# A two-layer graph attention kernel on one NeuronCore: layer 2's unit in another order (scores, hub values, turned exponentials, row turns)

## The chip, the cores and the metric

The kernel runs on one core of a Trainium2 chip. The metric is the device time of one execution in microseconds (us), the median of several. The engines are PE (TensorE, matmuls; PEld is its weight load), DVE (VectorE), ACT (ScalarE), POOL (GpSimd) and SP (SyncE, which here only issues DMAs). Each engine works through its own list of instructions in program order and waits on semaphores for the others.

## The reference

Eight graphs with the same 2048 nodes and the same links `adj`, 64 features a node. Two attention layers: in the first each of four heads maps x, in the second one head maps the leaky result. Each layer's scores are products of the mapped rows with themselves, masked by the links:

```python
mask = graph + jnp.eye(N) > 0
def gat(h, mask, b):                       # h: [..., N, D]
    s = jnp.where(mask, jnp.einsum('...nd,...md->...nm', h, h), -1e16)
    return jnp.einsum('...nm,...md->...nd', softmax(s), h) + b
h = jnp.einsum('bnc,hdc->bhnd', x, Wh)
z = leaky_relu(cat_heads(gat(h, mask, bh)), 0.2)
h2 = jnp.einsum('bnk,dk->bnd', z, Wo)
z2 = leaky_relu(gat(h2, mask, bo), 0.2)
out = (z2 - mu) * rsqrt(var + 1e-5) * gamma + beta
return layernorm(x + out)
```

## The kernel before, in words

The links are few: node 0 and its neighbours (the first 59 nodes, the "hub") have many, all others few. The other 1989 nodes are put into 153 sets of 13. For each set the kernel finds up to 128 nodes that any of its 13 members links to, and gathers just their rows from a table in HBM. Layer 1 does this from x, layer 2 from the table of second maps that layer 1 writes.

Layer 2 (lines 1319 to 1577) works in 39 units: unit 0 has one set, every other unit four. One pass of the loop `for u in range(-3, NU + 6)` is called unit u here. What it issues, in the order of the code:

- `values2` (line 1373, PE, "values"): the weighted sums of unit u, from the gathered rows and the masked weights `es2` (named share in the profile). Two units share a bank `o2`: the odd one begins it, the even one ends it.
- `gathers(u + LEAD)` (line 872, POOL): the indirect DMAs of the rows of unit u+9, into the buffers that the values of unit u have read. 36 buffers, four gathers a unit.
- the first part of `norm_sets` (lines 1401 and 1403, DVE), only after an even unit: reciprocals of the sums and the product. Its later parts (`spread`) go to fixed places of the next six units, either at `work_on(u, 0)` or at `work_on(u, 1)`: an odd unit gets leaky (1408), mean (1412), centring (1421), a variance (1436) and the products 1442, 1446, 1447; an even unit a mean, a centring, a product and a variance.
- `turn_scores(u + 1)` (line 1354, PE, "turned exponentials"): four transposes of the exponentials into the bank `turned_e`.
- `keep_scores(u + 1)` (line 1362, DVE, "masked weights"): the product of the turned exponentials and the links, into `es2`.
- `hub_step(k)` (PE 1174 the hub's scores, DVE 1183 the subtraction of its mask, ACT 1186 its exponentials, PE 1197 the hub's values of the step before). It has steps up to unit 5 only.
- `turn2(u + 3)` in two halves (line 560 on PE, "row turns", and line 1497 on ACT, "row copies"): each gathered row tile is transposed into one of three banks `t` and copied to `xts`.
- `scores2(u + 2)` between the halves (line 1343, PE, "scores", into `bank0`; line 1346, ACT, the exponentials `eT`). It reads the four row copies of unit u+2 and the own maps `bd`.
- `catch_up` (ACT): what the norms have left for ACT, the squares (1418) of the centred rows and the two steps of a reciprocal root (1428, 1429).
- `spread_own(u + 3)` (line 1137, ACT, "own maps"): two copies of the own nodes' maps into `bd`, at the unit's end.

SP loads the table of x + beta (1392) and stores the results, twelve DMAs a norm (1461). No planner sets the order: it is the order of the calls.

Of the kernel before, what the change touches and what calls it, by code (L numbers as in the profile page):

```python
# [361 lines left out]
def fast_kernel(ctx: ExitStack, tc: tile.TileContext, x, adj, Wh, bh, Wo, bo, gamma, beta, out, flag):  # L362
# [4 lines left out]
    H, D, _ = Wh.shape  # L367
# [17 lines left out]
    NHB = (NS + S10 - 1) // S10  # L385
# [38 lines left out]
    def half(k):  # L424
        return slice(k * 64, (k + 1) * 64)
# [4 lines left out]
    def sums(p):  # L430

        return slice(p * K1, (p + 1) * K1)
# [21 lines left out]
    NV = (NS + 7) // 8  # L454
# [152 lines left out]
    def hub_sets(b):  # L607

        return b * S10, min(S10, NS - b * S10)
# [254 lines left out]
    def pair(s):  # L864
        return 0 if s == NS - 1 else (s + 2) // 2
# [118 lines left out]
    def nodes(v, ap, tile):  # L984

        four = tile.rearrange("(t n) b d -> n t b d", n=32)
        for a in range(2):
            s = 8 * v + 4 * a
            w = min(4, NS - s)
            if w <= 0:  # L990
                continue
            for t in range(4):
                p0 = t * 32 + a * SET
                rest = ap[2 * (t % 2) + t // 2::4, BASE:, :].rearrange("f (k s) c -> k f s c", s=NS)[1:, :, s:s + w, :]
                yield (tile[p0 + 1:p0 + SET].rearrange("p (f w) c -> p f (w c)", f=2)[:, :, :w * D],
                       rest.rearrange("k f s c -> k f (s c)"))
            for s1, node, n in firsts(s, w):
                for t in range(2):
                    k0 = s1 - s
                    yield (four[a * SET][2 * t:2 * t + 2].rearrange("u (f w) c -> u f (w c)", f=2)[:, :, k0 * D:(k0 + n) * D],  # L1000
                           ap.rearrange("(f u v) n c -> v u f (n c)", f=2, u=2)[t, :, :, node * D:(node + n) * D])
# [112 lines left out]
    def one(name, tag):  # L1114
        return psum1.tile([P, 2, 512], F32, tag=tag, name=name)
# [4 lines left out]
    NU = (NS + 3) // 4  # L1120
# [3 lines left out]
    def side(u):  # L1124
        return (u - 1) % 2 if u else 0
# [6 lines left out]
    def spread_own(u):  # L1132

        w = len(sets[u])
        for p in range(2):
            src = own[half(p), :, sets[u][0] * SET:(sets[u][0] + w) * SET]
            nc.scalar.copy(bd[u % 3][half(p), :w, :, 16 * p:16 * p + SET], src.rearrange("c q (k n) -> c k q n", k=w))
# [27 lines left out]
    def hub_scores2(k, sp):  # L1165
        b = hub_order[k]
        n = BASE if b == NHB else hub_sets(b)[1] * SET
        held["sh", k] = sp
        for q in range(Q):
            if b == NHB:  # L1170
                keys = ownh[:, q // 2, q % 2 * HUB:q % 2 * HUB + n]
            else:
                keys = own[:, q, b * S10 * SET:b * S10 * SET + n]
            nc.tensor.matmul(sp[:n, q * 2 * HUB:(q + 1) * 2 * HUB], keys, ownb[:, q, :, :].rearrange("c p n -> c (p n)"),
                             start=True, stop=True)

    def hub_lift2(k):
        b = hub_order[k]
        n = BASE if b == NHB else hub_sets(b)[1] * SET
        sp = held.pop(("sh", k))  # L1180
        e = esh[k % 2]
        m = maskh[:n, 0, :].rearrange("p (k h) -> p k h", h=H)[:, :, 0] if b == NHB else maskt[:n, b, :]
        nc.vector.tensor_tensor(e[:n, :Q * 2 * HUB].rearrange("p (a n) -> p a n", a=2 * Q),
                                sp[:n, :Q * 2 * HUB].rearrange("p (a n) -> p a n", a=2 * Q),
                                m.unsqueeze(1).to_broadcast([n, 2 * Q, HUB]), OP.subtract)
        nc.scalar.activation(e[:n, :Q * 2 * HUB], e[:n, :Q * 2 * HUB], AF.Exp, bias=shifts[:n, 1:2], scale=1.0)

    def hub_values2(k):
        b = hub_order[k]
        first, last = k == 0, k == NHB  # L1190
        n = BASE if b == NHB else hub_sets(b)[1] * SET
        e = esh[k % 2]
        rw = rows.pop(("h", k))
        for q in range(Q):
            for p in range(2):
                c0 = (2 * q + p) * HUB
                nc.tensor.matmul(oh2[half(p), q * W2 + p:q * W2 + p + K1], e[:n, c0:c0 + 64], rw[:n, q, sums(p)],
                                 start=(first and q == 0), stop=last, skip_group_check=True)

    def hub_step(k, sp):  # L1200
        if k <= NHB:
            hub_scores2(k, sp)
            hub_lift2(k)
        if 0 < k <= NHB + 1:
            hub_values2(k - 1)

    def clear_esh():
        for k in range(2):
# [9 lines left out]
    for i in range(-3, NG + 3):  # L1218
        if 0 <= i + 1 < NG:
            sp = one(f"s{i + 1}", "S")  # L1220
# [17 lines left out]
        if 0 <= i < NG:  # L1238
            op = one(f"o{i}", "O")
# [5 lines left out]
        if NG - LOOK <= i < NG - 1:  # L1245
            for j in range(2):
                k = 2 * (i - NG + LOOK) + j
# [65 lines left out]
    def bank2(name, tag, bufs=1):  # L1313
        return psum2.tile([P, 2, 512], F32, tag=tag, name=name, bufs=bufs)
# [6 lines left out]
    def bank1(name):  # L1321
        return psum2.tile([P, 512], F32, tag="T", name=name, bufs=3)
# [13 lines left out]
    def scores2(u):  # L1336

        w = len(sets[u])
        sp = bank[0].rearrange("p (k n) -> p k n", k=4)
        for k, s in enumerate(sets[u]):  # L1340
            xt = held["T", 2, pair(s)].rearrange("c j (q n) -> c j q n", q=Q)
            for q in range(Q):
                nc.tensor.matmul(sp[q * 32:(q + 1) * 32, k, :], bd[u % 3][:, k, q, :], xt[:, s % 2, q, :], start=True, stop=True,  # L1343
                                 tile_position=(0, q * 32))
        e = held["E", u] = late.tile([P, 4, P], F32, tag="eT", name=f"eT{u}", bufs=2)
        nc.scalar.activation(e[:, :w], sp[:, :w], AF.Exp, bias=shifts[:, 1:2], scale=1.0)
# [109 lines left out]
    def norm_sets(v, op):  # L1456
        w = min(4, NS - 8 * v)

        def store(y):
            for src, dst in nodes(v, out, y):  # L1460
                nc.sync.dma_start(out=dst, in_=src)  # L1461

        view = op[:, :, :4 * W2].rearrange("p f (w c) -> p f w c", w=4)[:, :, :w]
        return norm(f"s{v}", v, view[:, :, :, 1:1 + D], view, 2 * w, store, NV - 4 <= v < NV - 2)
# [12 lines left out]
    def spread(u, parts, ahead=True):  # L1477

        for k, part in enumerate(parts):
            for t in range(2):  # L1480
                at = jobs.setdefault((u + k, t), [])
                if k == 0 and ahead:
                    at[:0] = part[t]
                else:
                    at.extend(part[t])
# [37 lines left out]
    k = 9  # L1523
    spread_own(0)
    for u in range(-3, NU + 6):
        if 0 <= u < NU:
            a = side(u)
            if a == 0:
                op = bank2(f"o2_{u}", "O")
            values2(op, sets[u], es2[a], a, len(sets[u + 1]) if a == 0 and u else 0)  # L1530
            if u + LEAD < NU:
                gathers(u + LEAD)
            if u == 0:
                nc.vector.memset(es2[0][:, :, :1, SET:2 * SET], 0.0)
            if a == 1 or u == 0:
                parts = norm_sets((u - 1) // 2 if u else NV - 1, op)
                for job in parts[0][0]:
                    job()
                spread(u + 1, parts[1:], False)
        if u == NU - 1:  # L1540
            range_of(1, rall2)
            in_limits()
        if 0 <= u + 1 < NU:
            turn_scores(u + 1)
            a = side(u + 1)
            keep_scores(u + 1, a)
        if u in (NU, NU + 1, NU + 3):
            last = jobs.pop((u, 1), [])
            n = 1 if u == NU + 1 else len(last)
            jobs[u, 0] = last[:n] + jobs.get((u, 0), [])  # L1550
            jobs[u, 1] = last[n:]
            catch_up()
        work_on(u, 0)
        for _ in range(2 if u == -3 else 1):
            if k <= NHB + 1:
                hub_step(k, bank1(f"sh{k}") if k <= NHB else None)
                if 8 <= k - 1 and k + 5 <= NHB:
                    hub_block(k + 5, hrows[(k - 1 - 8) % 6])
                if k == NHB + 1:
                    spread(u + 2 - u % 2, norm_hub(oh2))  # L1560
                k += 1
        if u + 3 < NU:
            turn2(u + 3, sets[u + 3][:2])
        if 0 <= u + 2 < NU:
            scores2(u + 2)
        catch_up()
        if u + 3 < NU:
            turn2(u + 3, sets[u + 3][2:])
        work_on(u, 1)
        if 3 <= u + 3 < NU:  # L1570
            spread_own(u + 3)
        if u == -2:
            range_of(0, rall)
            lists_fit()
# [40 lines left out]
```

## Time and profile before

| what | us |
|---|---|
| median of 3 runs (lowest, highest) | 963.1 (962.69, 968.35) |
| span of the profiled execution, first to last instruction | 828.9 |
| what lies around it, against the median | 134.2 |
| layer 2, from the first gather to the end | 575.9 to 828.9 |

The page does not give the profiled execution's own device time; its span is set against the median. In a row of the timeline stand the start and the length in us, the engine, the line, the operation, output<-input, a shape and the count; in brackets the idle time of the engine just before it and what ended it. A row of the stretches has the length, then the busy time (and instructions) of PE, PEld, DVE, ACT and POOL, the granted clock of PE (1.00 is full), the busy share of the DMA engines and GB/s.

### The profile page before, as it was taken

How to read it: one execution, taken by the hardware profiler on the slowest of the kernel's cores; microseconds unless marked ns; L12 is line 12 of the kernel's file. 1: busy time of each engine (PE TensorE's matmuls, PEld its weight loads, DVE VectorE, ACT ScalarE, POOL GpSimd, SP SyncE). 2: the span in 40 equal slices, each digit the busy share in tenths (PEclk: the TensorE clock that was granted, in tenths of full speed). 3: DMA queues.
4: the chain of work that ended last, by engine and by line, in shares of the span. 5: the costliest groups of instructions: out<-in, count | busy, mean ns of one | idle time of the engine just before them, and what ended most of it. 6: DMA issues, size and time to landing. Idle time of an engine off the chain costs nothing.

```text
span 828.9 us, 40381 instructions
## 1 busy us (share of the span) xinstructions
PE 725.0 (87%) x17262; PEld 615.5 (74%) x17262; DVE 600.8 (72%) x1328; ACT 529.3 (64%) x1131; POOL 449.9 (54%) x620
## 2 busy tenths in 40 slices
PE   1998688889999999999999999998999899989820
PEld 1675457678788889898989889887787688877620
DVE  3446984568778877898767777764347999998883
ACT  0354445556666667667667667773667899988852
POOL 5455356456445455555545555512777777777600
PEclk9999999999999999999999999999999999999975
DMA  4988744343323333454545545532986667766621
GB/s 83 231 225 240 219 156 111 98 121 98 86 71 90 96 90 98 119 144 139 143 120 141 142 139 137 142 114 88 300 245 185 192 170 214 224 201 197 172 54 32
DMA packets 80262, 121.55 MB, mean 147 GB/s; under 512 B 34539, under 2 KB 50751, under 8 KB 80075
## 3 DMA queue, kind: packets, MB, share of 16 engines
q0 software_dynamic: 24752, 65.67, 29.4%
q1 hardware_dynamic: 50973, 52.11, 21.6%
q8 instruction: 138, 2.26, 1.1%
q10 hardware_dynamic: 4350, 1.10, 0.7%
q14 instruction: 49, 0.40, 0.2%
HBM read 116.81 MB, written 18.25 MB: 163 GB/s over the span
## 4 chain that ended last, share of the span: by engine, by line
PE 61%; DVE 13%; DMA 12%; ACT 5%; issue 4%; SPq 3%; POOL 1%; POOLq 0%; DVEq 0%; ACTq 0%
PE s L901 10%; PE o L927 10%; PE bank L560 8%; PE cat L886 6%; DMA raw<-in_adj_dram 4%; PE o L944 4%; PE cat L579 4%; PE cat L961 4%; PE t L560 3%; PE bank L1343 2%; SPq L1461 2%; PE cat L971 2%; PE o L1373 2%; DMA rows<-table,index 2%; DMA out_dram<-y_s 2%
## 5 line engine op out<-in xcount | busy, mean ns | idle before, releaser
L872 POOL DMA_INDIRECT g<-table,index x154 | 162.3, 1054 | 172.8 <-PE o L927 145.5
L872 POOL DMA_INDIRECT rows<-table,index x153 | 161.2, 1053 | 51.8 <-issue 18.6
L566 ACT ACTIVATE z<-cat,bhp 128x208 f32<-128x208 f32 x154 | 58.4, 430 | 101.7 <-PE cat L579 101.7
L906 DVE TENSOR_TENSOR e<-s,mask 128x832 f32<-128x832 f32 x77 | 78.6, 1020 | 28.4 <-PE s L901 27.6
L927 PE MATMUL o<-g,e 128*64 128x65 f32 x2464 | 92.3, 226 | 5.6 <-issue 5.5
L560 PE MATMUL t<-ident,rows 128*128 128x128 f32 x612 | 86.1, 278 | 10.0 <-DMA rows<-table,index 4.7
L560 PE MATMUL bank<-ident,g 128*128 128x128 f32 x616 | 92.3, 273 | 1.5 <-DVE e L1106 1.2
L927 PEld LDWEIGHTS o<-g,e 128*64 128x64 f32 x2464 | 80.1, 138 | 17.1 <-issue 6.9
L901 PE MATMUL s<-y,xTg 64*64 64x52 f32 x4928 | 88.7, 220 | 0.0
L901 PEld LDWEIGHTS s<-y,xTg 64*64 64x64 f32 x4928 | 78.9, 134 | 12.9 <-issue 12.9
L1497 ACT COPY xts<-t 128x512 f32<-128x512 f32 x153 | 82.2, 583 | 7.0 <-PE t L560 6.0
L1235 ACT COPY xTg<-bank 128x512 f32<-128x512 f32 x154 | 82.6, 596 | 2.4 <-PE bank L560 2.4
L560 PEld LDWEIGHTS t<-ident,rows 128*128 128x128 f32 x612 | 66.5, 140 | 23.0 <-issue 9.9
L913 ACT ACTIVATE e<-e,shifts 128x832 f32<-128x832 f32 x77 | 78.4, 1019 | 2.0 <-DVE e L906 2.0
L742 POOL TENSOR_SCALAR a<-raw 117x1024 bf16<-117x1024 int32 x34 | 38.7, 1140 | 71.5 <-DMA raw<-in_adj_dram 49.1
L560 PEld LDWEIGHTS bank<-ident,g 128*128 128x128 f32 x616 | 73.5, 140 | 4.9 <-issue 1.3
L657 ACT ACTIVATE e<-e,shifts 128x960 f32<-128x960 f32 x32 | 35.1, 1096 | 54.7 <-DVE e L654 49.0
L886 PE MATMUL cat<-xo,gram 128*128 128x208 f32 (+1 forms) x304 | 66.3, 341 | 0.8 <-issue 0.8
L951 ACT COPY otb<-o 128x208 f32<-128x208 f32 x154 | 43.8, 335 | 22.0 <-ACT y L892 10.9
L654 DVE TENSOR_TENSOR e<-sh,maskh 128x960 f32<-128x960 f32 x32 | 36.9, 1154 | 26.6 <-PE sh L650 17.2
L935 DVE TENSOR_TENSOR osb<-o,rall 128x512 f32<-128x512 f32 x77 | 53.2, 692 | 2.7
L934 DVE RECIPROCAL rall<-o 64x8 f32<-64x8 f32 x154 | 31.5, 204 | 31.7 <-PE o L927 30.2
(198 smaller groups left out, 1488.0 us busy)
## 6 DMA issues: line engine op xcount, KB each, us to landing
raw<-in_adj_dram SPq DMA_DIRECT2D x34, 432.0 KB
xr_s<-table SPq DMA_DIRECT2D x19, 256.0 KB
table<-x SPq DMA_DIRECT2D x16, 260.0 KB
table<-rowt SPq DMA_DIRECT2D x152, 26.4 KB
out_dram<-y_s SPq DMA_DIRECT2D x152, 24.0 KB
x<-in_x_dram SPq DMA_DIRECT2D x24, 128.0 KB
table<-xb SPq DMA_DIRECT2D x11, 256.0 KB
table<-share SPq DMA_DIRECT2D x10, 256.0 KB
```

The source lines that it names most:

```text
L560: nc.tensor.transpose(tp[:, q * P:(q + 1) * P], rows[:, q, 1:1 + P], ident)
L566: nc.scalar.activation(z[:, hp], cat[:, :, hp * n:(hp + 1) * n], AF.Identity, bias=bhp[:, hp:hp + 1], scale=1.0)
L872: nc.gpsimd.indirect_dma_start(out=t.rearrange("n q c -> n (q c)"), out_offset=None, in_=table, in_offset=bass.IndirectOffsetOnAxis(ap=ind ...
L886: nc.tensor.matmul(cat[:, k, :n], gram[:, g % 2 * 2 + k, :], held["x", g // 2][:, :n], start=True, stop=True)
L901: nc.tensor.matmul(sp[half(r), p, (q * 2 + j) * M:(q * 2 + j + 1) * M], xt[half(p), j, q, half(r)], y[half(p), (j * Q + q) * M:(j * Q + q ...
L906: nc.vector.tensor_tensor(e[:, :16 * M].rearrange("p (a q n) -> p a q n", a=2, q=Q), sp[:, :, :8 * M].rearrange("p a (q n) -> p a q n", q= ...
L913: nc.scalar.activation(e[:, :16 * M], e[:, :16 * M], AF.Exp, bias=shifts[:, 0:1], scale=1.0)
L927: nc.tensor.matmul(op[half(p), j, o0:o0 + K1], e[:, c0:c0 + 64], rw[j][:, q, sums(p)], start=True, stop=True)
L935: nc.vector.tensor_tensor(osb, v[:, :, :, 1:K1], r.unsqueeze(3).to_broadcast([P, 4, 2, D]), OP.mult)
L951: nc.scalar.copy(ot.rearrange("c h (p w n) -> c p h w n", p=2, w=4)[:, p], v[:, :, p * 64:p * 64 + M].rearrange("c w (n h) -> c h w n", h=H))
L1235: nc.scalar.copy(t[:, k, :], bank[k])
L1497: nc.scalar.copy(xts[pair(s) % 4][:, s % 2, :], tp)
```

## The change

`hub_step` is split into `hub_after` (scores and exponentials) and `hub_before` (values of the step before). In a unit the own maps now come at the beginning, the scores right behind the values, the hub's values next, then the norm's first part, the turned exponentials, the hub's scores, and the four row turns last, with `catch_up` still between their halves. What is computed stays the same.

```diff
-    def hub_step(k, sp):
+    def hub_before(k):
+        if 0 < k <= NHB + 1:
+            hub_values2(k - 1)
+
+    def hub_after(k, sp):
         if k <= NHB:
             hub_scores2(k, sp)
             hub_lift2(k)
-        if 0 < k <= NHB + 1:
-            hub_values2(k - 1)
+
+    def hub_step(k, sp):
+        hub_after(k, sp)
+        hub_before(k)
...
     for u in range(-3, NU + 6):
+        if 3 <= u + 3 < NU:
+            spread_own(u + 3)
...
-            if a == 1 or u == 0:
-                parts = norm_sets((u - 1) // 2 if u else NV - 1, op)
-                for job in parts[0][0]:
-                    job()
-                spread(u + 1, parts[1:], False)
+        if 0 <= u + 2 < NU:
+            scores2(u + 2)
+        n_hub = 2 if u == -3 else 1
+        if n_hub == 1:
+            hub_before(k)
+        if 0 <= u < NU and (a == 1 or u == 0):
+            parts = norm_sets((u - 1) // 2 if u else NV - 1, op)
+            for job in parts[0][0]:
+                job()
+            spread(u + 1, parts[1:], False)
...
         if u + 3 < NU:
             turn2(u + 3, sets[u + 3][:2])
-        if 0 <= u + 2 < NU:
-            scores2(u + 2)
         catch_up()
         if u + 3 < NU:
             turn2(u + 3, sets[u + 3][2:])
         work_on(u, 1)
-        if 3 <= u + 3 < NU:
-            spread_own(u + 3)
```

PE in unit 21, from its values to the next unit, before (`o2_21` is the bank of units 21 and 22, `bank0` that of the scores, `t2_92` the turn of set 92):

```order
L1373 MATMUL o2_21_13856<-rows2_9_11230,share0_85 32x65 x8
L1373 MATMUL o2_21_13856<-rows2_10_11231,share0_85 32x65 x8
L1373 MATMUL o2_21_13856<-rows2_11_11232,share0_85 32x65 x8
L1373 MATMUL o2_21_13856<-rows2_12_11233,share0_85 32x65 x8
L1354 MATMUL turned_e_11257<-ident_78,eT22_13821 128x128 x4
L560 MATMUL t2_92_13909<-ident_78,rows2_21_11242 128x128 x4
L560 MATMUL t2_93_13915<-ident_78,rows2_22_11243 128x128 x4
L1343 MATMUL bank0_1919<-xts1_11212,share4_89 32x128 x8
L1343 MATMUL bank0_1919<-xts2_11213,share4_89 32x128 x8
L560 MATMUL t2_94_13943<-ident_78,rows2_23_11244 128x128 x4
L560 MATMUL t2_95_13949<-ident_78,rows2_24_11245 128x128 x4
```

And now:

```order
L1379 MATMUL o2_21_13858<-rows2_9_11230,share0_85 32x65 x8
L1379 MATMUL o2_21_13858<-rows2_10_11231,share0_85 32x65 x8
L1379 MATMUL o2_21_13858<-rows2_11_11232,share0_85 32x65 x8
L1379 MATMUL o2_21_13858<-rows2_12_11233,share0_85 32x65 x8
L1349 MATMUL bank0_1919<-xts1_11212,share4_89 32x128 x8
L1349 MATMUL bank0_1919<-xts2_11213,share4_89 32x128 x8
L1360 MATMUL turned_e_11257<-ident_78,eT22_13797 128x128 x4
L560 MATMUL t2_92_13929<-ident_78,rows2_21_11242 128x128 x4
L560 MATMUL t2_93_13935<-ident_78,rows2_22_11243 128x128 x4
L560 MATMUL t2_94_13945<-ident_78,rows2_23_11244 128x128 x4
L560 MATMUL t2_95_13951<-ident_78,rows2_24_11245 128x128 x4
```

The scores have moved ahead of the turned exponentials and of the first two row turns. (Lines behind the hub's functions have numbers higher by 6 in the changed kernel.)

ACT in unit 21 before, from the first two row copies to the own maps (`eT23` are the exponentials of the scores above, `var0_s8` a root, `sq0_s9` squares):

```order
L1497 COPY xts3_11214<-t2_92_13909 128x512
L1497 COPY xts3_11214<-t2_93_13915 128x512
L1346 ACTIVATE eT23_13937<-bank0_1919,shifts_117 128x512
L1428 ACTIVATE var0_s8_13852<-var0_s8_13852,shifts_117 128x8
L1429 ACTIVATE var0_s8_13852<-var0_s8_13852 128x8
L1418 ACTIVATE sq0_s9_13941<-y_s9_13779 128x512
L1497 COPY xts0_11211<-t2_94_13943 128x512
L1497 COPY xts0_11211<-t2_95_13949 128x512
L1137 COPY share2_87<-own_103 64x16x13 x2
```

And now:

```order
L1137 COPY share2_87<-own_103 64x16x13 x2
L1352 ACTIVATE eT23_13919<-bank0_1919,shifts_117 128x512
L1503 COPY xts3_11214<-t2_92_13929 128x512
L1503 COPY xts3_11214<-t2_93_13935 128x512
L1434 ACTIVATE var0_s8_13854<-var0_s8_13854,shifts_117 128x8
L1435 ACTIVATE var0_s8_13854<-var0_s8_13854 128x8
L1424 ACTIVATE sq0_s9_13943<-y_s9_13799 128x512
L1503 COPY xts0_11211<-t2_94_13945 128x512
L1503 COPY xts0_11211<-t2_95_13951 128x512
```

The own maps and the exponentials stand ahead of the row copies; root and squares still stand ahead of the last two row copies. On DVE, POOL and SP the instructions stand in the same order as before.

More of the change, by code (lines that the diff above doesn't have):

```diff
@@ L1553, in fast_kernel @@
         work_on(u, 0)
-        for _ in range(2 if u == -3 else 1):
+        for _ in range(n_hub):
             if k <= NHB + 1:
-                hub_step(k, bank1(f"sh{k}") if k <= NHB else None)
+                if n_hub > 1:
+                    hub_step(k, bank1(f"sh{k}"))
+                else:
+                    hub_after(k, bank1(f"sh{k}") if k <= NHB else None)
                 if 8 <= k - 1 and k + 5 <= NHB:
```

## The prediction

> **What bounds the kernel now.** I read the stages first (busy time by stretch), then the row gathers, then who waits for whom, then the order of time over one pair of units. Layer 2 runs from about 576 to 829 us of a span of 828.9.
>
> ```profile
> 640.00:740.00 100.00, 93.24 (x2308) 78.00 (x2302) 94.43 (x169) 88.05 (x207) 78.06 (x73) 1.00 0.70 200
> 740.00:784.00 44.00, 38.74 (x934) 31.67 (x929) 36.98 (x65) 34.98 (x80) 33.96 (x32) 1.00 0.68 192
> 780.00:800.00 20.00, 12.04 (x358) 9.38 (x358) 18.69 (x38) 12.94 (x35) 3.26 (x4) 0.91 0.34 90
> ```
>
> The columns after the length are PE, PEld, DVE, ACT, POOL, the clock, DMA. From 640 to 740 DVE (94.43 of 100) and PE (93.24) are both nearly full; from 740 both fall back, so something else is waited for. It is the gathers:
>
> ```profile
> L872 POOL DMA_INDIRECT rows<-table,index x122: 949/1007/1423, 615.0 to 782.4; - x122
> 782.40 1.01 POOL L872 DMA_INDIRECT rows<-table,index  x1 [0.30 <-issue]
> 741.95 1.37 PE L560 MATMUL t<-ident,rows 128*128 128x128 f32 x8 [1.03 <-DMA rows<-table,index]
> 786.53 0.63 PE L560 MATMUL t<-ident,rows 128*128 128x128 f32 x4 [0.82 <-DMA rows<-table,index]
> ```
>
> POOL issues 122 gathers between 615.0 and 782.4, 1.38 us apart (167.4 / 121) or 5.53 for the four of a unit, whatever PE does. PE is quicker, uses up its lead by 742 and then waits for rows. So there are two limits in turn, and which one a change meets decides it. The unit's own pace on PE, where nothing is waited for, is values to values:
>
> ```profile
> 683.10 1.22 PE L1373 MATMUL o<-rows,share 128*32 128x65 f32 x64
> 684.24 0.66 PE L1354 MATMUL turned_e<-ident,eT 128*128 128x128 f32 x4
> 684.74 1.04 PE L560 MATMUL t<-ident,rows 128*128 128x128 f32 x8
> 685.70 1.08 PE L1343 MATMUL bank<-xts,share 128*32 128x128 f32 x32
> 686.72 1.09 PE L560 MATMUL t<-ident,rows 128*128 128x128 f32 x8
> 687.74 1.11 PE L1373 MATMUL o<-rows,share 128*32 128x65 f32 x64
> ```
>
> That is 4.64 us, so 9.28 for a pair. DVE's work comes in pairs of units: an odd unit (A) and an even one (B). One pair, as DVE runs it, with ACT and PE at its end:
>
> ```profile
> 699.21 0.58 DVE L1362 TENSOR_TENSOR share<-turned_e,maskh 128x416 f32<-128x416 f32 x1
> 701.15 0.69 DVE L1421 SCALAR_TENSOR_TENSOR y_s<-st_s,y_s 128x512 f32<-128x512 f32 x1
> 702.73 0.69 DVE L1442 TENSOR_TENSOR y_s<-y_s,var_s 128x512 f32<-128x512 f32 x1 [0.30 <-ACT var_s L1429]
> 704.79 0.42 DVE L1401 RECIPROCAL rall<-o 64x8 f32<-64x8 f32 x2
> 705.85 0.58 DVE L1362 TENSOR_TENSOR share<-turned_e,maskh 128x416 f32<-128x416 f32 x1
> 707.06 0.69 DVE L1421 SCALAR_TENSOR_TENSOR y_s<-st_s,y_s 128x512 f32<-128x512 f32 x1
> 707.78 0.63 ACT L1418 ACTIVATE sq_s<-y_s 128x512 f32<-128x512 f32 x1 [0.33 <-DVE y_s L1421]
> 708.32 1.05 ACT L1497 COPY xts<-t 128x512 f32<-128x512 f32 x2
> 709.11 0.59 DVE L1362 TENSOR_TENSOR share<-turned_e,maskh 128x416 f32<-128x416 f32 x1 [0.16 <-PE turned_e L1354]
> 709.26 0.78 ACT L1137 COPY share<-own 64x208 f32<-64x208 f32 x2
> 710.09 1.08 PE L1343 MATMUL bank<-xts,share 128*32 128x128 f32 x32 [0.29 <-ACT share L1137]
> 711.10 1.09 PE L560 MATMUL t<-ident,rows 128*128 128x128 f32 x8
> ```
>
> From the masked weights of A (L1362, 699.21) to those of the next A (709.11) are 9.90 us, with 0.30 and 0.16 idle: DVE is the limit here. Mark the ACT rows: the squares (L1418) wait for the centred rows of DVE (L1421), and the last two row copies (L1497) stand behind the squares.
>
> **The change part by part.** No instruction is added or removed. On DVE, POOL and SP none changes its place; PE and ACT are reordered.
>
> *Own maps first.* Before, the scores wait for the own maps (L1137), which stand behind the last row copies:
>
> ```profile
> PEld bank L1343 <- ACT share L1137: 9.8, 20, 0.7
> PE bank L1343 <- ACT share L1137: 5.4, 13, 0.5
> ACT eT L1346 <- PE bank L1343: 6.1, 16, 1.0
> ```
>
> These waits go: 5.4 us on PE. The two copies cost 0.78 in their new place, where ACT idles ahead of the exponentials anyway (6.1 us); without that cover they would delay the exponentials, which nobody needs before the next unit. But the last row copies are what the scores really need, and that wait stays, and comes sooner.
>
> *Scores right behind the values.* The scores of unit u+2 used to start 2.60 us after the values of unit u (683.10 to 685.70); now 1.05 after. They need all four row copies of the unit before: one wait for each set of 32x128 products, so three quarters of the 1.01 us (710.09 to 711.10) can run early and the last quarter, 0.25, waits for the last copy. Until it has run, the turned exponentials behind it on PE wait too, and with them DVE's masked weights. Before, the turned exponentials stood ahead of the scores and waited for nothing on ACT. This closes a loop: DVE's centred rows of B, squares, two copies, last quarter, turned exponentials, masked weights of A, and DVE again up to the centred rows of B.
>
> ```profile
> 783.05 0.59 DVE L1362 TENSOR_TENSOR share<-turned_e,maskh 128x416 f32<-128x416 f32 x1 [0.55 <-PE turned_e L1354]
> 782.35 0.65 PE L1354 MATMUL turned_e<-ident,eT 128*128 128x128 f32 x4
> ```
>
> The loop, start to start: masked weights A to B 6.64 less the wait of 0.30 is 6.34 (705.85 - 699.21); to the centring 1.21; to the squares 0.72; to the copies 0.54; the two copies 1.05; from their end to the scores 0.05 (as 710.04 to 710.09); the quarter 0.25; turned exponentials to masked weights 0.70 (782.35 to 783.05). Sum 10.86 us a pair. The other half, A to B, is looser: through ACT the weights of B could start 5.25 us after those of A (centring 1.94, then 0.72, 0.54, 1.05, 0.05, 0.25 and 0.70 as above), and DVE gets there only after 6.34. So the pair goes from 9.90 to 10.86 where DVE set the pace, and nearly equals the gathers' 11.07 where they did. PE, with 9.28 of its own, then waits about 1.6 us a pair, queued behind the scores' last quarter; behind it wait the row turns, whose rows are there early. Later values free the gathers' buffers later, but a gather is nine units ahead of them: the last ones, about 778, need the values of unit 29, which come some 15 us sooner than that even when they are 15 us late.
>
> *Hub values between, row turns last.* The hub's steps end in unit 5. There the hub's subtraction stands behind a whole centring on DVE, and all four row copies stand behind its exponential:
>
> ```profile
> 612.28 1.14 PE L1373 MATMUL o<-rows,share 128*32 128x65 f32 x64
> 614.04 0.59 DVE L1362 TENSOR_TENSOR share<-turned_e,maskh 128x416 f32<-128x416 f32 x1 [4.30 <-PE turned_e L1354]
> 614.76 0.69 PE L1197 MATMUL bank<-hrows,share 117*64 117x65 f32 x16
> 615.37 1.09 PE L560 MATMUL t<-ident,rows 128*128 128x128 f32 x8
> 617.95 1.05 ACT L1497 COPY xts<-t 128x512 f32<-128x512 f32 x2
> 619.47 0.30 ACT L1428 ACTIVATE var_s<-var_s,shifts 128x2 f32<-128x2 f32 x1
> 620.43 1.05 ACT L1497 COPY xts<-t 128x512 f32<-128x512 f32 x2
> 627.25 0.59 DVE L1362 TENSOR_TENSOR share<-turned_e,maskh 128x416 f32<-128x416 f32 x1 [3.03 <-PE turned_e L1354]
> ```
>
> In unit 3 the weights come 1.05 + 1.01 + 0.61 (hub values) + 0.70 = 3.37 after 612.28: 615.65. From there the copies start 3.91 later as now (614.04 to 617.95); then two copies 1.05, root and squares 0.96 (619.47 to 620.43), two copies 1.05, then 0.05 and 0.25: 622.9. Unit 4 is PE's own 6.0 (its 4.64 and the hub's 0.61 and 0.8), then 0.61 and 0.70: the weights of unit 5 at 630.2 against 627.25, so +3.0. The bounds of this term: 0, if unit 4 regains it, and 5. Four turns in a row on three banks are free: the fourth needs the first copy done. The norm's first step behind the scores costs nothing, since DVE's order is as before.
>
> *The sum.* From the weights of unit 5 (627.25) to those of unit 35 (783.05) the kernel took 155.8 us for 15 pairs. Now 15 x 10.86 = 162.9, and the hub rows' normalisation, which is on DVE's part of the loop:
>
> ```profile
> 638.08 0.43 DVE L1408 SCALAR_TENSOR_TENSOR y_h<-y_h 128x256 f32<-128x256 f32 x1
> 663.07 0.41 DVE L1436 TENSOR_REDUCE var_h<-sq_h 128x4 f32<-128x256 f32 x1
> ```
>
> About ten such rows of 0.43, 4.5 us. So 167.4, that is +11.6; with +3.0 from the hub's units +14.6. Behind unit 35 the end is a run of DVE work and then stores, unchanged in order, and it shifts as a whole. The profiled execution lies 134.2 us under the median of 963.1 by its span of 828.9 (launch and what surrounds it, unchanged): **963.1 + 14.6 = 977.7**, say 978. The unknown is how finely the scores wait: if the whole block stands still until the last copy, 0.76 more a pair, 11.4 in all, 989; if the squares come earlier than DVE's rows say, the loop loosens down to the gathers' limit, 964. I take the quarter, since each set has its own wait in the program's order.
>
> **The rivals.** *The gathers set the end anyway, and nothing is lost.* For it: POOL's row, which never waits, and PE's 44 us from 740 with 5.3 idle. It holds if the loop takes no more than 155.8 / 15 = 10.39 a pair, hub rows included. Then the masked weights of unit 35 come only the 1.01 us of scores later: 964.1. Against: the sum is 10.86 from rows, and three quarters of the stretch lie before the gathers bind.
>
> *The whole block waits:* 989, above. Against it stand the sets' own waits.
>
> *The own maps' waits were the real loss:* 5.4 us back on PE, 957.7; at the utmost 9.8 (the weight loads' row), 953.3. Against: the last gather is issued at 782.40 in any case, and 786.53 was already its landing.
>
> *The clock falls* because PE idles about 0.8 us twice a pair. For it: the row for 780 to 800 has a clock of 0.91 with 8 us idle of 20. Against: 740 to 784, with 5.3 idle of 44, keeps 1.00. At 0.91 PE's own pair is 10.2, still under the loop; only PE's parts in the loop (0.95) and in the hub's units grow by a tenth, 0.1 a pair: 980. The Trainium skill, "TensorE: Matmul & The Clock Gate", section "Why this matters for your kernels", asks for no gaps of over about 3 us, since one such idle window brings the clock back to half. By that rule holes of 0.8 us change nothing; were the clock halved all the same, PE's pair would be 18.6 and the time, as an estimate from that page, 963.1 + 15 x (18.6 - 10.39) = 1086. No row here shows a half clock in this stage.
>
> **How the numbers follow.** Forecast (the loop) 0.66; gathers bind 0.20; whole block 0.08; own maps 0.04; clock 0.02. A measurement of this kernel can tell about 1%, 9.6 us. Of the loop's 0.66 about a tenth lies under +9.6 (hub term zero and some overlap). Slower: 0.60 + 0.08 + 0.02 = 0.70; within 1%: 0.06 + 0.20 + 0.02 = 0.28; faster 0.02. The range holds the gathers' case, with 3 us below it since the own maps' waits may come back in part, and the whole block: 961 to 989.
>
> **What would show it.** Right: a new group of waits of the scores (L1349) for the row copies (L1503) on PE, under 1 us each, about 30 of them; DVE waiting for the turned exponentials in odd units; 10.9 us a pair from unit 6 on; no wait of PE for gathered rows after 740; POOL unchanged at 1.38. Wrong: if PE still waits for rows near 786, or a pair before 740 takes less than 10.2, the loop isn't closed as I say.

## The result and the profile after

The changed kernel took 1009.4 us (median of four, 1002.0 to 1011.4) beside 965.7 us of the kernel before: 4.5% slower, ratio 1.0448, interval 1.0404 to 1.0492. The direction is the predicted one; the loss, 43.6 us, is three times the 14.6 of the sum.

One thing has to be known before any row is read. The same kernel before was run again with a profile, in several sets of runs, each set on one chip. In two sets it took 828 us, in the other five 966 to 974, and within a set the timed executions kept to one of the two (but for one execution of 1759 us beside the second slow set, which is not counted). Chip 4 gave 828.0 in one set and 966.6 in another, so it is not shown to be a trait of the chip; the texts on record say "quick chip" and "slow chip", and I keep the two words for the sets. The profile that the prediction read is of the quick kind, the times beside it of the slow kind. Where both are from one execution they agree: 827.2 us has a span of 825.4, 967.1 has 965.3, and here 1011.4 has 1009.4. Two microseconds lie around a span, not 134.

The stretches of the changed kernel (slow), in the middle of layer 2 and in its last units, and its gathers:

```profile
780.00:860.00 80.00, 58.20 (x1048) 38.80 (x1047) 41.54 (x71) 38.59 (x92) 38.02 (x38) 1.00 0.47 128
935.00:970.00 35.00, 28.90 (x708) 22.97 (x708) 29.70 (x54) 27.16 (x62) 0.00 (x0) 1.00 0.16 43
```

```profile
L872 POOL DMA_INDIRECT rows<-table,index x153: 949/1004/1216, 601.2 to 928.3; - x153
...
  PE o L1379: 123.8, 30
```

No engine is full: PE 58 of 80, DVE 42, at a granted clock of 1.00. POOL, which in the quick profile waited 4.6 us in all for the values before its gathers, waits 123.8 us here; in the slow profile of the kernel before, further down, it is 79.4. One unit of that stretch, 8.57 us long where the quick profile of before had 4.64 (PE, then who waits for it):

```profile
801.10 1.11 PE L1379 MATMUL o<-rows,share 128*32 128x65 f32 x64
801.30 0.63 ACT L1424 ACTIVATE sq_s<-y_s 128x512 f32<-128x512 f32 x1
802.03 0.79 PE L1349 MATMUL bank<-xts,share 128*32 128x128 f32 x5
803.14 0.43 PE L1349 MATMUL bank<-xts,share 128*32 128x128 f32 x3 [0.33 <-issue]
803.87 0.43 PE L1349 MATMUL bank<-xts,share 128*32 128x128 f32 x4 [0.30 <-issue]
804.61 0.87 PE L1349 MATMUL bank<-xts,share 128*32 128x128 f32 x20 [0.31 <-issue]
805.41 0.66 PE L1360 MATMUL turned_e<-ident,eT 128*128 128x128 f32 x4
805.91 0.80 PE L560 MATMUL t<-ident,rows 128*128 128x128 f32 x4
806.95 1.29 PE L560 MATMUL t<-ident,rows 128*128 128x128 f32 x8 [0.24 <-issue]
807.87 0.69 ACT L1352 ACTIVATE eT<-bank,shifts 128x512 f32<-128x512 f32 x1 [4.32 <-PE t L560]
808.45 1.06 ACT L1503 COPY xts<-t 128x512 f32<-128x512 f32 x2
809.08 0.66 PE L560 MATMUL t<-ident,rows 128*128 128x128 f32 x4 [0.84 <-ACT xts L1503]
809.67 0.55 PE L1379 MATMUL o<-rows,share 128*32 128x65 f32 x24
```

Two things to see. The 32 scores take 3.45 us (802.03 to 805.48) instead of 1.01, in pieces with "issue" between them: PE waits for nothing that the profile shows. (The ends of matmuls in a profile are modelled, so PE may also have worked longer than its records say.) And the fourth row turn waits 0.84 for the first row copy. The predicted loop isn't here: the squares (801.30) are done long before the scores need the copies behind them. It is in the last units, after the last gather (928.3):

```profile
937.39 1.11 PE L1379 MATMUL o<-rows,share 128*32 128x65 f32 x64
938.32 0.62 PE L1349 MATMUL bank<-xts,share 128*32 128x128 f32 x16
938.56 0.63 ACT L1424 ACTIVATE sq_s<-y_s 128x512 f32<-128x512 f32 x1 [0.89 <-DVE y_s L1427]
939.10 1.05 ACT L1503 COPY xts<-t 128x512 f32<-128x512 f32 x2
939.72 0.91 PE L1349 MATMUL bank<-xts,share 128*32 128x128 f32 x16 [0.78 <-ACT xts L1503]
940.56 0.66 PE L1360 MATMUL turned_e<-ident,eT 128*128 128x128 f32 x4
941.26 0.59 DVE L1368 TENSOR_TENSOR share<-turned_e,maskh 128x416 f32<-128x416 f32 x1 [1.53 <-PE turned_e L1360]
...
948.28 0.93 PE L1379 MATMUL o<-rows,share 128*32 128x65 f32 x50
```

A pair, 937.39 to 948.28, takes 10.89 us there; the prediction had 10.86.

### The profile page after: what moved, and what is told of

Same layout as the page of the kernel before. It is cut to its first block, busy times and chain, and to the rows that moved or that the text cites. A ratio compares the mean times of both kernels' runs of the same rounds, so it can differ in the third digit from the quotient of the medians.

```text
span 1009.4 us, 40381 instructions
## 1 busy us (share of the span) xinstructions
PE 806.0 (80%) x17262; PEld 649.2 (64%) x17262; DVE 603.5 (60%) x1328; ACT 527.9 (52%) x1131; POOL 442.2 (44%) x620
## 2 busy tenths in 40 slices
DMA packets 80262, 121.55 MB, mean 120 GB/s; under 512 B 34539, under 2 KB 50751, under 8 KB 80075
## 4 chain that ended last, share of the span: by engine, by line
PE 64%; DVE 10%; issue 7%; DMA 6%; ACT 5%; another core or an unknown queue 5%; SPq 1%; POOL 0%; DVEq 0%; ACTq 0%; POOLq 0%
PE s L901 9%; PE o L927 8%; PE bank L560 7%; PE bank L1349 6%; PE t L560 5%; PE cat L886 5%; PE cat L579 3%; PE o L944 3%; DMA raw<-in_adj_dram 3%; PE cat L961 3%; PE o L1379 3%; PE turned_e L1360 2%; PE cat L971 2%; ACT xts L1503 2%
## 5 line engine op out<-in xcount | busy, mean ns | idle before, releaser
L872 POOL DMA_INDIRECT g<-table,index x154 | 161.9, 1051 | 198.0 <-PE o L927 171.0
L872 POOL DMA_INDIRECT rows<-table,index x153 | 154.7, 1011 | 178.9 <-PE o L1379 123.8
L560 PE MATMUL t<-ident,rows 128*128 128x128 f32 x612 | 91.0, 280 | 33.5 <-ACT xts L1503 21.0
L1349 PE MATMUL bank<-xts,share 128*32 128x128 f32 x1224 | 86.8, 280 | 37.5 <-issue 30.4
L901 PE MATMUL s<-y,xTg 64*64 64x52 f32 x4928 | 103.6, 223 | 2.6 <-issue 1.9
L901 PEld LDWEIGHTS s<-y,xTg 64*64 64x64 f32 x4928 | 91.2, 135 | 18.2 <-issue 16.6
L1368 DVE TENSOR_TENSOR share<-turned_e,maskh 128x416 f32<-128x416 f32 (+1 forms) x39 | 22.7, 583 | 122.1 <-PE t L560 79.5
L1352 ACT ACTIVATE eT<-bank,shifts 128x512 f32<-128x512 f32 (+1 forms) x39 | 26.5, 679 | 121.2 <-PE t L560 82.9
L1349 PEld LDWEIGHTS bank<-xts,share 128*32 128x32 f32 x1224 | 42.1, 109 | 74.2 <-issue 63.2
```

The source lines that it names most:

```text
L560: nc.tensor.transpose(tp[:, q * P:(q + 1) * P], rows[:, q, 1:1 + P], ident)
L872: nc.gpsimd.indirect_dma_start(out=t.rearrange("n q c -> n (q c)"), out_offset=None, in_=table, in_offset=bass.IndirectOffsetOnAxis(ap=ind ...
L901: nc.tensor.matmul(sp[half(r), p, (q * 2 + j) * M:(q * 2 + j + 1) * M], xt[half(p), j, q, half(r)], y[half(p), (j * Q + q) * M:(j * Q + q ...
```

## The experiments

Two theories. **Loop**: as predicted, through DVE's centring, the squares, the row copies, the scores and the turned exponentials. **Supply**: on a slow chip PE is short of something that the profile doesn't name, and what the change costs there hangs on PE's order, not on the loop. Ratios are against the kernel before in the same set, with their interval.

| kernel | quick | slow |
|---|---|---|
| changed | 847.2, 1.0246 (1.0195 to 1.0298) | 1006.8, 1.0406 (1.0352 to 1.0460) |
| changed, squares behind all copies | 828.7, 1.0000 (0.9961 to 1.0039); 826.9, 0.9992 (0.9967 to 1.0017) | 1002.2, 1.0360 (1.0285 to 1.0434) |
| scores behind values alone | 885.3, 1.0686 (1.0607 to 1.0765) | |
| own maps first alone | 825.7, 0.9952 (0.9919 to 0.9985) | 973.2, 1.0004 (0.9969 to 1.0038) |
| changed, turned exponentials ahead of scores | | 997.0, 1.0307 (1.0243 to 1.0370); 998.4, 1.0316 (1.0247 to 1.0385) |
| changed, hub's steps as before | | 1006.9, 1.0381 (1.0322 to 1.0440); 1009.6, 1.0416 (1.0340 to 1.0492) |
| changed, fourth bank | | 986.6, 1.0202 (1.0159 to 1.0246) |
| before, interleaved, own maps first | | 964.8, 0.9977 (0.9955 to 1.0000) |
| changed, fourth bank, squares behind | | 992.4, 1.0207 (1.0152 to 1.0262) |

**The kernel before again**, three profiles.

> The kernel before, unchanged, so that its profile comes from the same day and chip as the others. The profile that the prediction used has a span of 828.9 us, while the time was 963 to 969 us; the changed kernel's profile has a span of 1009.4 us beside a time of 1011.4. If launch costs 134 us (as the prediction took it), the span is 829 again. If the earlier profile is of an execution that ran otherwise than the timed ones, the span is 961 to 967, and the missing 134 us stand inside it: in a unit of layer 2 of 7 to 8 us instead of 5.1, and in a hole of some 25 to 40 us of PE at the border of the layers, both with PE waiting for nothing that the profile shows.

827.2 us, span 825.4. Neither case: only 2 us lie around the span, and this set was quick.

> The kernel before once more, for a profile of it beside the changed one on the same chip. Where a run of it takes about 829 us: PE waits for nothing unnamed in layer 2, a pair of units takes 9.5 to 10. Where it takes about 965: supply theory says that it too shows PE waiting for nothing that the profile shows, in layer 2 and at the border of the layers, with a unit of 7 to 8 us; if the slower chip slows something else (the clock, the gathers' landing), those rows stand there instead.

833.8 us, quick again.

> The kernel before, for its profile beside the others of this call. On a slow chip (966 us): supply theory says units of 7 to 8 us while the gathers run, with PE waiting for nothing that the profile shows, and a hole at the border of the layers as in the changed kernel; if instead its units take about 5 us and the 137 us lie elsewhere, the changed kernel's units of 8.6 us are the change's doing. On a quick chip: 826 to 835.

967.1 us, slow. Its own rows, one stretch and one unit:

```profile
724.00:885.00 161.00, 131.38 (x2442) 91.90 (x2441) 104.09 (x181) 93.27 (x216) 92.00 (x84) 0.98 0.52 141
```

```profile
762.45 1.11 PE L1373 MATMUL o<-rows,share 128*32 128x65 f32 x64
763.50 0.81 PE L1354 MATMUL turned_e<-ident,eT 128*128 128x128 f32 x4
764.58 0.53 PE L560 MATMUL t<-ident,rows 128*128 128x128 f32 x3 [0.27 <-issue]
...
766.02 1.35 PE L1343 MATMUL bank<-xts,share 128*32 128x128 f32 x26
767.64 0.45 PE L1343 MATMUL bank<-xts,share 128*32 128x128 f32 x5 [0.27 <-issue]
768.41 0.27 PE L1343 MATMUL bank<-xts,share 128*32 128x128 f32 x1 [0.31 <-issue]
768.61 1.27 PE L560 MATMUL t<-ident,rows 128*128 128x128 f32 x8
```

So the kernel before has the same unnamed gaps, 7.35 us for this unit. From the values of unit 8 to those of unit 29 its units take 7.65 on average on the slow chip (724.50 to 885.12) and 5.12 on the quick one (636.50 to 743.94). The changed kernel takes 8.70 (740.45 to 923.16) and 5.61 (643.05 to 760.92). The hole at the border of the layers is in both slow profiles too, 23.6 us before and 15.2 in one wait after (7.6 at most in the changed kernel's second slow profile), and is no part of the change:

```profile
641.01 1.95 PE L1174 MATMUL sh<-share,own 128*117 128x120 f32 x8 [23.61 <-DVE share L1183]
```

```profile
637.22 0.70 PE L1197 MATMUL bank<-hrows,share 117*64 117x65 f32 x8 [15.17 <-issue]
```

Where the two kernels part, by the starts of values in the slow profiles of before and after (44.1 us in all): 7.6 ahead of unit 0, which in the changed kernel's second slow profile was 2.8, so mostly chance; 8.4 in units 0 to 7; 22.1 in 8 to 28; 4.4 in 29 to 35; 1.6 behind. In the quick profiles (17.8 us between the spans): 0.6, 6.0, 10.4, -0.2 and 1.0.

**The changed kernel again.**

> The changed kernel, unchanged, once more, because the kernel before took 828.8 us in the first runs and 966 us beside the changed one: the chips are not the same. On a chip where the kernel before takes about 829: loop theory 840 to 855 (10.9 us a pair, at most 11.6 if the whole block of scores waits), with the scores waiting for the row copies and PE waiting for nothing unnamed; supply theory 860 to 870 (the same 4.5%), with PE waiting for nothing that the profile shows. On a chip where it takes about 965: 1000 to 1012 again.

1006.8: slow, as expected of that kind, which tells nothing between the theories.

> The changed kernel beside the two others of this call. Where before takes about 829: loop theory 840 to 855, supply theory 860 to 870. Where before takes about 965: 1000 to 1012.

847.2 on a quick chip: the loop's range. There PE has no unnamed wait among its units; its only wait of size in units 8 to 35 is the predicted one, for the row copies, and DVE's only one is for the turned exponentials, in the odd units:

```profile
PE bank L1349 <- ACT xts L1503: 18.7, 26, 1.9
PE o L1379 <- DVE share L1368: 1.1, 1, 1.1
DVE share L1368 <- PE turned_e L1360: 20.7, 14, 1.5
```

No wait for gathered rows is left there, and the last gather is issued at 775.4, in the kernel before at 776.8.

**The loop cut.**

```diff
             turn2(u + 3, sets[u + 3][:2])
-        catch_up()
         if u + 3 < NU:
             turn2(u + 3, sets[u + 3][2:])
+        catch_up()
```

> The changed kernel with the squares and roots of ACT moved behind all four row copies, so that the scores never stand behind DVE's centring. Loop theory (as predicted: centring, squares, copies, scores, turned exponentials, masked weights): the loop is cut, and the time falls back to 960 to 970. Supply theory (PE gets its instructions too slowly once values and scores stand behind each other, and the gathers' traffic makes it worse): the order on PE is that of the changed kernel, so the time stays at 1000 to 1012.

> The changed kernel with the squares and roots behind all four row copies, on the chip of this call. It took the time of the kernel before where that is 829. Where before takes about 965: loop theory 960 to 972; supply theory (PE's order is that of the changed kernel) 1000 to 1012.

Quick: 828.7 and 826.9, the kernel before's time. PE's order is the changed kernel's, only ACT's squares and roots have moved: on a quick chip cutting the loop gives the whole loss back, and the supply theory falls there. It does not undo the loss unit by unit. By the starts of values units 0 to 4 still take 36.4 us (36.5 in the changed kernel, 30.9 before), and units 5 to 34 take 147.6, less than the 156.4 of the kernel before, with DVE nearly full:

```profile
643.00:746.70 103.70, 95.31 (x2438) 82.72 (x2436) 99.62 (x180) 92.62 (x219) 80.54 (x77) 1.00 0.71 202
```

Whether the kernel before would gain as much from the squares' new place was not tried.

> The changed kernel with the loop cut (squares and roots behind all four row copies). On a slow chip: loop theory 960 to 972; supply theory, since PE's order is that of the changed kernel, 1000 to 1012; both at work, 980 to 995. On a quick chip: 825 to 832, as it was.

Slow: 1002.2. The loop theory falls there. Against the changed kernel's 1006.8 in another set 4.6 us are gone, which the two intervals alone could not tell, but the starts of values say where: from unit 30 to 36 it takes 28.6 us (928.73 to 957.32) instead of 32.6 (932.11 to 964.69), which is the loop of the last units; units 8 to 28 stay at 8.73.

**The parts alone.**

```diff
+        if 0 <= u + 2 < NU:
+            scores2(u + 2)
         if u == NU - 1:
...
             turn2(u + 3, sets[u + 3][:2])
-        if 0 <= u + 2 < NU:
-            scores2(u + 2)
```

> The kernel before with one part alone: the scores directly behind the values; the own maps stay at the unit's end, the hub's steps stay as they were. Loop theory and supply theory both put the loss on this part: 995 to 1012. If the loss is at the border of the layers (the hub's order, the units -3 to 0), it is 960 to 985 here.

885.3, on a quick chip, where the numbers were meant for a slow one; as a ratio, 1.0686, it is above what either theory gave. The own maps, still last, lie in the loop as well, and the scores wait for them once in each of 30 units, up to 3.3 us:

```profile
PE bank L1343 <- ACT share L1137: 55.2, 30, 3.3
```

(Units 6 to 35.) The changed kernel, with the own maps first (and the hub's values in another place), takes 847.2 on a quick chip, so most of these waits are gone there.

```diff
     for u in range(-3, NU + 6):
+        if 3 <= u + 3 < NU:
+            spread_own(u + 3)
...
         work_on(u, 1)
-        if 3 <= u + 3 < NU:
-            spread_own(u + 3)
```

> The kernel before with the other part alone: the own maps at the unit's beginning, everything else as before. Loop theory: 957 to 966 (5.4 us of waits of the scores go, the end is set by the gathers). Supply theory: no change, 960 to 970. If this part is what costs, because the own maps now stand ahead of the exponentials and of the row copies on ACT: over 975.

825.7: 0.5% faster (0.8 to 0.2%), by less than the 1% that one kernel's measurement tells.

> The kernel before with the own maps at the unit's beginning, alone. On a quick chip it took 825.7 beside 828.8 (0.9952). On a slow chip, where the scores wait for the own maps only 1.5 us in 21 units: no change, 963 to 970; if the copies in the new place delay what PE waits for there, over 972.

973.2 beside 974.5: nothing on a slow chip.

**The order on PE.** The turned exponentials ahead of the scores, then the hub's steps as before:

```diff
-        if 0 <= u + 2 < NU:
-            scores2(u + 2)
         n_hub = 2 if u == -3 else 1
...
             keep_scores(u + 1, a)
+        if 0 <= u + 2 < NU:
+            scores2(u + 2)
```

> The changed kernel with the turned exponentials (and DVE's masked weights) ahead of the scores again, both still ahead of the four row turns. Loop theory: DVE's weights no longer stand behind the row copies, so the time is that of the kernel before, within 1% (820 to 835 where before takes 829). Supply theory: values and scores are parted by four transposes only, so half of the loss or more stays (840 or more, where before takes 829).

> The changed kernel with the turned exponentials ahead of the scores, which takes the masked weights out from behind the row copies. On a quick chip: loop theory 822 to 834; if scores waiting on PE cost by themselves, 836 to 847. On a slow chip 993 to 1001, as it was.

997.0 and 998.4, both slow: 8 to 10 us of the loss go, and most stays. Units 8 to 28 take 8.74 (736.75 to 920.33), as in the changed kernel; the loop's last units are quicker. Four transposes between values and scores leave the pace of these units as it was.

```diff
-        if n_hub == 1:
-            hub_before(k)
...
+                hub_step(k, bank1(f"sh{k}") if k <= NHB else None)
```

> The changed kernel with the hub's steps as they were before (scores, exponentials and values of the step before in one place, behind the turned exponentials). The prediction priced the hub's new order at 3.0 us, 0 to 5: so this is 0 to 5 us below the changed kernel. If the hub's order at the border of the layers is what costs, it is at the kernel before's time, within 1%.

> The changed kernel with the hub's steps as before. On a quick chip the changed kernel took 847.2; the hub's order was priced at 3.0 us, 0 to 5: so 842 to 847. On a slow chip 1001 to 1010, as it was.

1006.9 and 1009.6, both slow: the hub's order costs nothing there that can be told. On a quick chip it wasn't tried.

**A fourth bank for the row turns.** What was left was the fourth turn. PE's waits from unit 8 to 29, first before, then changed (its first profile), both slow:

```profile
PE bank L1343 <- issue: 14.6, 42, 1.0
PE t L560 <- issue: 8.5, 32, 1.1
```

```profile
PE bank L1349 <- issue: 20.2, 64, 0.4
PE t L560 <- ACT xts L1503: 15.6, 20, 1.3
PE t L560 <- issue: 6.9, 20, 1.0
```

```diff
-            tp = bank1(f"t2_{s}")
+            tp = bank[1] if u >= 12 and s == sets[u][3] else bank1(f"t2_{s}")
```

> The changed kernel, with a fourth bank for the row turns from unit 9 on (the hub's, which is free by then), so that no row turn waits for a row copy. Nothing else moves. On a slow chip (before 968): if the fourth turn's wait of 0.8 us a unit is a cause, 26 units x 0.8 = 21 us go: 982 to 990. If PE is only short of instructions and waits there instead of elsewhere: 1000 to 1012. On a quick chip (before 828) the loop sets the pace and the turns never wait: 843 to 852 either way.

986.6: the ratio to the kernel before goes from 1.0406 to 1.0202, so 20 of some 40 us are gone, as expected if that wait is a cause. From unit 10 to 29 the units take 7.66 (752.31 to 897.80), the kernel before's pace, though the unnamed waits among the scores are still there (PE's waits in those 19 units):

```profile
PE bank L1349 <- issue: 17.0, 52, 0.6
PE t L560 <- issue: 4.2, 17, 0.4
PE o L1379 <- DVE share L1368: 3.6, 6, 1.0
```

> The kernel before with the own maps at the unit's beginning and, from unit 6 on, one row turn in the middle of the values and one in the middle of the scores, so that dense runs of small matmuls are halved. If dense runs cost PE its supply on a slow chip, PE's unnamed waits shrink: 925 to 955 where before takes 968. If the supply is a rate that no order on PE changes: 962 to 975. On a quick chip (before 828): 820 to 832, since DVE and the gathers set the pace.

```diff
         for k, s in enumerate(sets):
+            if k == 2 and between:
+                between()
...
+                    (lambda: turn2(u + 3, sets[u + 3][:1])) if early else None)
...
+            scores2(u + 2, (lambda: turn2(u + 3, sets[u + 3][1:2])) if early else None)
```

One row turn stands inside `values2` and one inside `scores2`, behind their second set, from unit 6 on. 964.8: parting PE's dense runs in this way gains nothing, although the scores' unnamed waits halve (7.3 us over about the same units against 14.6):

```profile
PE bank L1345 <- issue: 7.3, 24, 0.4
PE o L1377 <- issue: 3.4, 10, 0.5
```

The units stay at 7.71 (725.77 to 887.68). That three kernels with three orders end at 7.65 to 7.71 speaks for a floor of about that size on a slow chip, to which a wait of PE is added; that is argued, not shown, and what would set the floor is open.

Both edits, the fourth bank and the squares behind all copies, together:

> The changed kernel with the fourth bank and with the squares behind all four row copies. On a slow chip (before 967): if the two causes add, 986.6 less the 4.7 us that cutting the loop gave there (1006.8 to 1002.2) = 982, range 978 to 986; if the fourth bank already took all that can be had, 984 to 990. On a quick chip (before 828): the loop is cut, 823 to 831.

992.4, in a set in which the kernel before took 974.5: ratio 1.0207 against 1.0202 with the fourth bank alone. That the two causes add isn't borne out, at an uncertainty of half a per cent each; the expected 982 was missed. The profile, of its quickest execution (985.4), shows why in part: units 29 to 35 take 35.2 us instead of 41.6 with the fourth bank alone, so the loop is cut there, but units 10 to 28 take 7.83 each instead of 7.66, 3.3 us in all; why these are longer is open.

No kernel beat the one before by more than 1%.

## Why the prediction was right or wrong

**The step that failed** is in the sum: "The profiled execution lies 134.2 us under the median of 963.1 by its span of 828.9 (launch and what surrounds it, unchanged)". Around a span lie 2 us. The 134 were inside the timed executions: longer units of layer 2 (7.65 instead of 5.12, some 53 us in the 21 units from 8 on, and 20 more in units 0 to 7), the hole at the border, and a longer layer 1. So every price was read from an execution in which PE has no unnamed waits in layer 2, and added to the time of one in which it has many.

**The loop** was right where its rows hold. On quick chips a pair takes 10.89 against 10.86, DVE's weights of the odd unit wait for the turned exponentials, the scores for the copies, and cutting the loop brings the time back to that of the kernel before. The loss there is 19.2 us, 14.6 in the sum. The terms, by the starts of values in the two quick profiles: units 5 to 34 grow by 10.3 (156.4 to 166.7), near the 11.6 of pairs and hub rows together; units 0 to 4, the hub's, by 5.6 instead of 3.0, a little above the bound of 5, and they keep that when the loop is cut; what is behind by 1. On slow chips, as long as gathers run, units are longer than the loop (17.4 a pair against 10.9), and it is worth 4 to 5 us in the last units. So a loss was rightly forecast for the timed executions, but in the main by luck: most of their loss has another cause.

**"Four turns in a row on three banks are free: the fourth needs the first copy done"** failed. I named the wait and didn't measure its slack. In the quick profile of the changed kernel the fourth turn starts 0.09 us behind the end of the first copy in 20 of the 21 units from 8 to 28, and those that wait on a slow chip start 0.05 behind it, so next to nothing is left; in units 0 to 7 PE waits for row copies even on a quick chip, 2.8 us in 5 waits where it was 1.0 in 2. On a slow chip the copies start late, behind exponentials that themselves start 2.4 us after the scores (805.48 to 807.87), and the wait is 0.8 us a unit. That is the largest cause shown, 20 of some 40 us: with the fourth bank units 8 to 28 take 161.9 us, beside 182.7 in the changed kernel and 160.6 before. Of the remaining 19 between the two profiles 4.5 lie in units 29 to 35, which is the loop, and 9.4 in units 0 to 7 (75.7 against 66.3), where the fourth bank wasn't yet in use. There the row turns wait 3.8 us for the row copies (1.2 before) and 2.4 for the hub's mask (1.0), and the unnamed waits among the scores are 9.4 us where they were 1.4. Why PE's scores are held up there was not settled.

**Own maps first:** costing them at nothing was right on both kinds. The rival that put the gain at 5.4 us saw 3.2 on a quick chip when they were moved alone.

**The rivals:** the whole block of scores doesn't wait, as said: half of it runs ahead (the sum had three quarters), and the 0.78 is for the rest. The clock wasn't it, 1.00 in the slow units with holes of 0.3 to 0.8 us. As a loss the range ran from -2 to +26 us: it holds the 19.2 of the quick chip, and on a slow one the 20 that the fourth bank leaves, but not the 43.6. None of the rivals was an execution unlike the profiled one, and none gave the fourth turn a price.

## What to carry to other kernels

Set the span of the profile beside the time first: a gap of 16% isn't launch until an execution shows both numbers, and prices from such a profile hold as ratios of that execution at best. When a reordering is "free" because something is ready in time, measure how much in time: a slack of under 0.1 us is gone as soon as one engine runs late. And a cause found in one trace (the loop; cutting it gave 19 us back) need not be the cause of the loss that was timed.

## What the runs showed of the hardware

The same kernel ran at two paces, 828 and 966 to 974 us, at granted clocks of 0.97 and 0.94 on average. On the slow one PE has waits that nothing in the profile releases, mostly while the row gathers run, and others see PE's results late: 2.4 us above, where on the quick chip the exponentials start 0.2 behind the scores. The DMA queues carried the same, 80,262 packets of 121.55 MB in both, and the instruction blocks, quick and slow, were the same number with about the same time: 1.1% of 825.4 us and 1.0% of 965.3 us on 16 engines are both about 150 us for 138 blocks.

```profile
span 825.4 us, 40381 instructions
...
q8 instruction: 138, 2.26, 1.1%
```

```profile
span 965.3 us, 40381 instructions
...
q8 instruction: 138, 2.26, 1.0%
```

The Trainium skill, "Runtime: NRT & Kernel Launch", section "Instruction fetch mechanics", has each engine's instructions streamed in 16 KiB blocks by its own DMA queue and calls the cost mostly hidden; the blocks' equal time agrees with that, and does not explain PE's waits. Another page of the Trainium skill, "NOTIFIC — the notification-queue block", section "Overflow: three behaviours, one of which stalls the engine", says that the unit which writes the profiler's records holds engines back when its own pipeline fills. All runs here were profiled, and 34,524 of the 40,381 instructions are PE's, so that would fit, but no run here shows it, and the quick executions left records of just as many instructions. What sets the pace stays open.
